# Summing softmax weights on GpSimd into one buffer per step, and single tiles on TensorE in gaps

## The chip, the cores and the metric

The kernel runs on one core of one Trainium2 chip. A core has engines that run side by side, each through its own list of instructions in order: TensorE (PE, matrix multiplication; its weight loads are shown apart as PEld), VectorE (DVE), ScalarE (ACT), GpSimd (POOL) and SyncE (SP, which here only issues DMA transfers). They wait for one another through semaphores. The metric is the device time of one execution in microseconds (us).

## The reference: what is computed

One pre-norm transformer layer in float32, for x of 2 x 2048 x 512:

```python
x = x + attention(layernorm(x))          # 16 heads of 32, rotary q and k, causal
x = x + ffn(layernorm(x))

# attention
scores = einsum('bhqd,bhkd->bhqk', q, k) / sqrt(dk)      # causal mask
attn   = softmax(scores, axis=-1)
ctx    = einsum('bhqk,bhkd->bhqd', attn, v)
return ctx @ Wo.T

# ffn: a base product, and 8 low-rank experts of rank 16, of which a router takes 2 per token
result = x @ base_w.T + base_b
gate   = top-2 of softmax(x @ router_w.T + router_b), renormalised
return result + 2.0 * sum over experts of gate * (x @ A_e) @ B_e
```

The change concerns the denominator of the softmax: for each query, the sum of exp(score - shift) over all keys.

## The kernel before

The 4096 tokens are cut into 8 blocks of 512 queries: blocks 0 to 3 are the first batch, 4 to 7 the second, and a block's place in its batch is j = 0 to 3. The heads come in 4 groups of four. A *step* is one block and one group (n, g), 32 in all. A step of place j has 4(j+1) tiles of 128 keys.

For one step, `row_maxima` first multiplies queries by keys in one orientation (tiles `sm`, L367) and VectorE takes the largest score of every query (`pm`, L375 and L380). Then `attend` multiplies keys by queries (tiles `sc`, L463), subtracts the maxima by a small multiplication (L471), and ScalarE writes the exponentials, the *weights*, into a tile buffer `pt` of 128 keys x 4 heads x 512 queries (L485). On the diagonal GpSimd sets the weights of later keys to zero (`affine_select`, L494). `weighted` (L519) multiplies weights by values into `av`. Of the four diagonal tiles, the second and the fourth share one buffer.

The denominator is made in two moves. When two neighbouring tiles both have had their `av` multiplication, GpSimd adds the second tile into the first (L534), in two halves of two heads. Three phases later (or two, in a gap) `summed` (L545) lets TensorE multiply the pair by a matrix of ones into the PSUM tile `den`. So a step of place j has 2(j+1) groups of four such multiplications, the last of them half as wide. After the last, ScalarE copies `den` out, the sums go through DRAM to spread them over partitions, VectorE takes reciprocals, and GpSimd multiplies them into `ctx` (L581).

Order. TensorE, ScalarE and VectorE run in the order in which the program writes their instructions; GpSimd and SP are ordered by the framework's scheduler. The program goes by *phases*. While the weights of one step are computed, the maxima of the next are computed beside them (`side_by_side`): one phase holds half of a weights tile and half of a maxima tile, or, where no maxima are left, a whole weights tile. After each phase `between` issues what is due (`av` two phases after the scores, `den` groups), then a list of other work is served: projections with their rotation (`project`, L185, L198 to L201), values (L210), and for finished blocks the output projection, router and feed-forward (`finish`, L239, L265, L320, L327). If a phase gave TensorE no such filler, `ahead` issues a `den` group early. The last step has no maxima beside it, and after it only the last block's `finish` remains.

`PTS = 4` buffers hold weights tiles; `before` sees to it that what reads the oldest has been issued. PSUM has six score banks in turn. `wo` and `base_w` (1 MB each) are loaded once and stay in SBUF.

Of the kernel before, what the change touches and what calls it, by code (L numbers as in the profile page):

```python
# [15 lines left out]
P = 128  # L16
# [5 lines left out]
BLK = 512  # L22
# [4 lines left out]
LORA_SCALING = 32.0 / 16.0  # L27
THETA = 10000.0
MASKED = -1e30
PTS = 4  # L30
SWAP = [i ^ 1 for i in range(32)]


# [1 line left out]
def preln_attention_moe_lora(  # L35
# [26 lines left out]


    et = mybir.EngineType
    ctx.enter_context(tc.manual_schedule(engines={et.PE, et.Activation, et.DVE}))


    banks = [0]
# [26 lines left out]

    blocks = [(b, j) for b in range(B) for j in range(NB)]

    def load_x(n, t, keep):
        b, j = blocks[n]
        if keep:  # L100
            xt = wide.tile([P, D], F32, tag="x", bufs=4, name=f"xf_{n}_{t}")
        else:
            xt = p2.tile([P, D], F32, tag="tmp", bufs=5, name=f"xa_{n}_{t}")
        nc.sync.dma_start(out=xt, in_=x[bass.ds(b * S + j * BLK + t * P, P), :])
        return xt
# [18 lines left out]
    wq = load_weight(wq_t, "wq")  # L124
    first_turn = load_turn(0)
    wv = load_weight(wv_t, "wv")
    wo = load_weight(wo_t, "wo")
    exp_in = load_weight(expert_in, "exp_in")
    bias_sb = const.tile([P, D + E], F32, name="bias_sb")
    nc.sync.dma_start(out=bias_sb, in_=bias.to_broadcast([P, D + E]))  # L130
    base_w = load_weight(base_wt, "base_w")
    exp_out = const.tile([ER, D], F32, name="exp_out")
    nc.sync.dma_start(out=exp_out, in_=expert_out)

    def moments(xt, t, name):

        n6, n2 = nc.vector.BN_STATS_DIM, nc.vector.BN_AGGR_DIM
        made = small.tile([P, n6 + n2 + 2], F32, tag="mom", bufs=4, name=f"mom_{name}_{t}")
        st, mv = made[:, :n6], made[:, n6 : n6 + n2]
        rstd, shift = made[:, n6 + n2 : n6 + n2 + 1], made[:, n6 + n2 + 1 :]  # L140
        nc.vector.bn_stats(st, xt)
        nc.vector.bn_aggr(mv, st)
        nc.gpsimd.tensor_scalar_add(rstd, mv[:, 1:2], EPS)
        nc.gpsimd.tensor_tensor(rstd, rstd, power, ALU.pow)
        nc.gpsimd.tensor_scalar(shift, mv[:, 0:1], rstd, -1.0, ALU.mult, ALU.mult)
        return rstd, shift
# [11 lines left out]
    def prepare(n):  # L158
# [23 lines left out]
        def project(which, w, g):  # L182
            pj = bank(f"{which}ps_{n}_{g}")
            for c in range(NC):
                nc.tensor.matmul(  # L185
                    out=pj,
                    lhsT=w[:, c, bass.ts(g, P)],
                    rhs=held["xn_t"][:, c, :],
                    start=(c == 0),
                    stop=(c == NC - 1),  # L190
                )
            if which == "k":
                dest = kv.tile([P, BLK], F32, tag="k", name=f"k_{n}_{g}")
            else:
                dest = wide.tile([P, BLK], F32, tag="q", bufs=3, name=f"q_{n}_{g}")
            made[which].append(dest)
            sw = p2.tile([P, BLK], F32, tag="tmp", bufs=5, name=f"sw_{which}_{n}_{g}")
            nc.vector.stream_shuffle(sw, pj, SWAP)  # L198
            nc.vector.tensor_mul(dest, pj, held["turn"][0])
            nc.gpsimd.tensor_mul(sw, sw, held["turn"][1])  # L200
            nc.gpsimd.tensor_add(dest, dest, sw)  # L201

# [24 lines left out]
    def finish(n, ctx_t):  # L227
# [3 lines left out]

        def load(t):
            held["x"].append(load_x(n, t, True))

        def output(t):
            xt = held["x"][t]
            po = bank(f"ops_{n}_{t}")
            for c in range(NC):
                nc.tensor.matmul(  # L239
                    out=po,  # L240
                    lhsT=ctx_t[c][:, bass.ts(t, P)],
                    rhs=wo[:, c, :],
                    start=(c == 0),
                    stop=(c == NC - 1),
                )
            nc.vector.tensor_add(xt, po, xt)
            held["by"].append(moments(xt, t, f"f{n}"))

        def scaled(t):
            xt = held["x"][t]  # L250
            xn = p2.tile([P, D], F32, tag="tmp", bufs=5, name=f"xn_f{n}_{t}")
            normalise(xn, xt, held["by"][t])
            held["xn"].append(xn)
            nc.gpsimd.tensor_add(xt, xt, bias_sb[:, :D])

        def turned(t):
# [59 lines left out]
        def result(t):  # L316
            xt = held["x"][t]
            po = bank(f"yps_{n}_{t}")
            for c in range(NC):
                nc.tensor.matmul(  # L320
                    out=po,
                    lhsT=held["xn_t"][:, c, bass.ts(t, P)],
                    rhs=base_w[:, c, :],
                    start=(c == 0),
                    stop=False,
                )
# [90 lines left out]
    def between():  # L417
# [4 lines left out]
            due.pop(0)[2]()  # L422
        return many > 0

    def ahead():

        for i, entry in enumerate(due):
            if entry[0] - entry[3] <= phase[0]:
                return due.pop(i)[2]()


    def attend(s):

# [3 lines left out]
        tiles = NT * (j + 1)  # L437
        together = [(kt,) for kt in range(diagonal + 1)]
        together += [(diagonal + 1, diagonal + 3), (diagonal + 2,)]
        pts, index, paired = {}, {}, {}  # L440

        def low(kt):
            return max(kt - diagonal, 0) * P
# [7 lines left out]
        def quad(*kts):  # L451
# [23 lines left out]

            def weigh(r):
                if kts[0] not in pts:
                    pt = p2.tile(
                        [P, 4, BLK], F32, tag="pt", bufs=PTS, name=f"pt_{n}_{g}_{kts[0]}"
                    )  # L480
                    for kt in kts:
                        index[kt], pts[kt] = begun[0], pt
                    begun[0] += 1
                pt = pts[kts[0]]
                nc.scalar.activation(  # L485
                    pt[:, r, all_of], sc[r][:, all_of], AF.Exp, scale=1.0 / math.sqrt(DK)
# [1 line left out]
                if kts[0] >= diagonal and r % 2:  # L488
# [2 lines left out]
                    on = pt[:, r - 1 : r + 1, at : at + len(kts) * P]  # L491
                    if len(kts) > 1:
                        on = on.rearrange("p h (k q) -> p h k q", q=P)
                    nc.gpsimd.affine_select(  # L494
                        out=on, in_=on, compare_op=ALU.is_ge, fill=0.0, base=0,
                        pattern=[[0, 2]] + [[0, len(kts)]] * (len(kts) > 1) + [[1, P]],
# [2 lines left out]

            def before():  # L500

                while any(tile <= begun[0] - PTS for _, tile, _, _ in due):
                    due.pop(0)[2]()

            def after():

                oldest = diagonal + 1 if kts[0] == tiles - 2 else kts[0] - kts[0] % 2
                later(2, index[oldest], lambda: weighted(kts))

            return before, take, scores, shift, weigh, after  # L510

        def weighted(kts):
            if kts[0] == 0:
                s["av"] = ps_o.tile([P, BLK], F32, tag="av", name=f"av_{n}_{g}")
            for kt in kts:
                jj, tt = divmod(kt, NT)
                for r in range(4):
# [5 lines left out]
                        start=(kt == 0),  # L523
                        stop=(kt == tiles - 2),
                    )

            for kt in kts:
                kt -= kt % 2
                paired[kt] = paired.get(kt, 0) + 1
                if paired[kt] == 2:  # L530
                    lo = low(kt + 1)
                    for r in (0, 2):
                        some = pts[kt][:, r : r + 2, place(kt, lo)]
                        nc.gpsimd.tensor_add(some, some, pts[kt + 1][:, r : r + 2, place(kt + 1)])  # L534
                    later(3, index[kt], lambda kt=kt: summed(kt), 1)
            if kts[-1] == tiles - 2:
                s["dest"] = wide.tile([P, BLK], F32, tag="ctx", bufs=6, name=f"ctx_{n}_{g}")
                nc.scalar.copy(s["dest"], s["av"])

        def summed(kt):  # L540
            lo = low(kt)
            if kt == 0:
                s["den"] = ps_o.tile([P, BLK], F32, tag="den", name=f"den_{n}_{g}")
            for r in range(4):
                nc.tensor.matmul(  # L545
                    out=s["den"][DK * r : DK * r + DK, lo:],
                    lhsT=ones,
                    rhs=pts[kt][:, r, lo:],
                    start=(kt == 0),
                    stop=(kt == tiles - 2),  # L550
                )
            if kt == tiles - 2:
                total = p2.tile([P, BLK], F32, tag="tmp", bufs=5, name=f"sum_{n}_{g}")
                nc.scalar.copy(total, s["den"])
                if (n, g) == steps[-1]:
# [14 lines left out]
                    nc.sync.dma_start(out=few, in_=spread(sums))  # L570

                def over_sums():
                    if (n, g) != steps[-1]:
                        nc.vector.reciprocal(few, few)
                        nc.sync.dma_start(out=spread(over), in_=few)
                        for r in range(4):
                            nc.sync.dma_start(
                                out=total[DK * r : DK * r + DK, :],
                                in_=over[r : r + 1, :].to_broadcast([DK, BLK]),
                            )  # L580
                    nc.gpsimd.tensor_mul(s["dest"], s["dest"], total)  # L581
                    s["ctx"].append(s["dest"])

                if (n, g) == steps[-1]:
                    over_sums()
                else:
                    set_aside(phase[0] + 4, over_sums)

# [107 lines left out]

    def end_block(n):

        start = phase[0] + 6
        end = max(begin[NC * (n + 2)] - EARLY, start + 24)  # L700
        stages = finish(n, contexts[n])
        for i, stage in enumerate(stages):
# [7 lines left out]
    for step in steps + [None]:  # L710
# [18 lines left out]
        for i in range(slots):  # L729
# [2 lines left out]
            todo = part(maxima, i, slots), late if i == 0 else part(weights, i - 1, slots)  # L732
            for _ in side_by_side(*todo):
                phase[0] += 1
                given = between()
                if ending is not None and len(contexts[ending]) == NC:
                    end_block(ending)
                    ending = None
# [9 lines left out]
                while waiting and waiting[0][2] <= phase[0]:  # L748
# [9 lines left out]
                    free = us > 0.0 and free  # L758
                    do_stage(waiting.pop(0)[3])
                    credit -= us  # L760
                    given = given or us > 0.0
                if not given:
                    ahead()
        late = part(weights, slots - 1, slots)
        if step:
            split()
            before, turned = s, turned_next
    for _ in side_by_side([], late):
        phase[0] += 1
        between()  # L770
    while due:
        due.pop(0)[2]()
    while aside:
# [54 lines left out]
```

## Time and profile before

| | us |
|---|---|
| median of 3 runs | 1978.18 (1974.35 to 1980.91) |
| the profiled execution's own time | 1982.82 |
| its span in the profile | 1981.0 |
| mean granted TensorE clock | 0.987 of full speed |

| engine, idle before a group of instructions | us in all | times | longest |
|---|---|---|---|
| ACT, exponentials, for TensorE's scores | 882.0 | 475 | 7.3 |
| POOL, adds L534, for ScalarE's exponentials | 193.6 | 45 | 10.6 |
| POOL, adds L534, for TensorE's `av` | 140.0 | 48 | 6.7 |
| POOL, `ctx` product L581, for a transfer | 84.8 | 25 | 10.0 |
| PEld, loads for `av`, for masks L494 | 32.4 | 40 | 1.7 |
| PE, `av`, for masks L494 | 14.2 | 28 | 1.3 |

The span is what the profiler recorded from first to last instruction; the profiled execution is one execution, a little over the median. A matrix multiplication in float32 shows as two instructions on TensorE, so a group of four is eight. Matmuls are pipelined and their ends are modelled: the share of busy time counts overlapped and stretched instructions too. In a timeline a row gives start, length, engine, line, operation, what is written from what, how many, and in brackets the engine's idle time before it with what ended it.

### The profile page before, as it was taken

To read this page: it belongs to the slowest core of one execution; us is meant where nothing else is said; L and a number is where in the kernel's file an instruction comes from. 1 tells how busy PE (TensorE), PEld (TensorE's weight loads), DVE (VectorE), ACT (ScalarE), POOL (GpSimd) and SP (SyncE) were. 2 spreads that over 40 slices of the span, in tenths; PEclk is the share of its full clock that TensorE was granted. 3 is DMA by queue.
4 is the path that set the end of the run, shared out by engine and by line. 5 is a ranking of instruction groups with operands and counts; after the bars stand their busy time and mean duration, and the time that the engine had idled before them with its cause. 6 is when DMAs were issued, how large, how long until landed. Compare 5 with 4: busy or idle time off the path is not lost.

```text
span 1981.0 us, 31399 instructions
## 1 busy us (share of the span) xinstructions
PE 1918.0 (97%) x12256; PEld 731.2 (37%) x12256; DVE 1018.2 (51%) x2760; ACT 768.0 (39%) x1601; POOL 1008.7 (51%) x906
## 2 busy tenths in 40 slices
PE   7999999999999999999999999999999999999997
PEld 3433433333333333333343434333433333333333
DVE  3555555555554655553255546446565555555403
ACT  1323342344433444353532334224434334443451
POOL 3545554455464555355565345435555545553572
PEclk9999999999999999999999999989999999999999
DMA  5000110000100000100000001100011000001000
GB/s 186 23 12 13 32 35 22 7 7 28 60 1 7 7 1 18 48 23 8 10 28 12 28 28 38 49 7 7 2 38 49 1 6 7 1 7 44 6 7 22
DMA packets 34861, 46.33 MB, mean 23 GB/s; under 512 B 12956, under 2 KB 13468, under 8 KB 34712
## 3 DMA queue, kind: packets, MB, share of 16 engines
q1 hardware_dynamic: 34712, 44.32, 7.0%
q8 instruction: 96, 1.57, 0.3%
q14 instruction: 53, 0.43, 0.1%
HBM read 35.40 MB, written 8.90 MB: 22 GB/s over the span
## 4 chain that ended last, share of the span: by engine, by line
PE 83%; POOL 7%; issue 4%; DVE 4%; ACT 1%; DMA 1%; SPq 0%; POOLq 0%; DVEq 0%
PE sm L367 24%; PE av L519 13%; PE den L545 6%; PE ops L239 6%; PE vps L210 6%; PE qps L185 5%; PE kps L185 5%; PE yps L320 5%; PE sc L471 5%; PE sc L463 4%; POOL pt L534 3%; POOL pt L494 2%; PE mid L265 1%; PE yps L327 1%; ACT pt L485 1%
## 5 line engine op out<-in xcount | busy, mean ns | idle before, releaser
L485 ACT ACTIVATE pt<-sc 128x512 f32<-128x512 f32 (+1 forms) x1152 | 595.1, 572 | 950.8 <-PE sc L471 882.0
L534 POOL TENSOR_TENSOR pt<-pt,pt 128x1024 f32<-128x1024 f32 (+2 forms) x320 | 609.9, 1920 | 339.2 <-ACT pt L485 193.6
L463 PE MATMUL sc<-q,k 32*128 32x512 f32 (+3 forms) x2560 | 677.5, 576 | 10.7 <-DVE parts L392 10.1
L367 PE MATMUL sm<-k,q 32*128 32x512 f32 (+3 forms) x2560 | 644.1, 574 | 6.3 <-POOL q L201 3.6
L380 DVE TENSOR_REDUCE pm<-sm 128x1 f32<-128x512 f32 x768 | 490.8, 685 | 286.5 <-PE sm L367 273.6
L367 PEld LDWEIGHTS sm<-k,q 32*128 32x128 f32 x2560 | 221.4, 184 | 375.0 <-issue 148.7
L519 PE MATMUL av<-pt,v 128*32 128x512 f32 (+3 forms) x2560 | 306.0, 550 | 19.1 <-POOL pt L494 14.2
L375 DVE CUSTOM_DVE_ANT_0 sm<-sm,mask 128x128 f32<-128x128 f32 (+3 forms) x512 | 245.8, 512 | 141.8 <-PE sm L367 118.7
L471 PE MATMUL sc<-max,ones_b 3*128 3x512 bf16 (+3 forms) x1280 | 261.2, 346 | 0.0
L463 PEld LDWEIGHTS sc<-q,k 32*128 32x128 f32 x2560 | 233.1, 185 | 51.2 <-issue 24.2
L494 POOL TENSOR_SCALAR_AFFINE_SELECT pt<-pt 128x256 f32<-128x256 f32 (+1 forms) x192 | 93.0, 485 | 154.7 <-ACT pt L485 152.2
L545 PE MATMUL den<-pt,ones 128*32 128x512 f32 (+1 forms) x1280 | 163.3, 569 | 0.0
L519 PEld LDWEIGHTS av<-pt,v 128*32 128x32 f32 x2560 | 57.5, 109 | 201.5 <-issue 142.1
L185 PE MATMUL kps<-xnt_a,wk 128*128 128x512 f32 x256 | 123.3, 626 | 5.0 <-ACT xnt_a L156 4.9
L239 PE MATMUL ops<-wo,ctx 128*128 128x512 f32 x256 | 120.2, 614 | 2.7 <-POOL ctx L581 2.7
L320 PE MATMUL yps<-base_w,xnt_f 128*128 128x512 f32 x256 | 116.9, 599 | 2.6 <-DVE pm L380 1.6
L185 PE MATMUL qps<-xnt_a,wq 128*128 128x512 f32 x256 | 118.3, 605 | 0.0
L210 PE MATMUL vps<-wv,xnt_a 128*128 128x512 f32 x256 | 117.5, 604 | 0.0
L471 PEld LDWEIGHTS <-ones_b 3*128 3x128 bf16 x1280 | 78.3, 94 | 101.0 <-issue 94.5
L200 POOL TENSOR_TENSOR sw_q<-sw_q,sin 128x512 f32<-128x512 f32 x32 | 40.7, 1273 | 112.5 <-DVE sw_q L198 112.5
L200 POOL TENSOR_TENSOR sw_k<-sw_k,sin 128x512 f32<-128x512 f32 x32 | 40.7, 1273 | 109.2 <-DVE sw_k L198 93.8
L581 POOL TENSOR_TENSOR ctx<-ctx,sum 128x512 f32<-128x512 f32 x32 | 40.6, 1268 | 90.1 <-DMA sum<-over 84.8
(85 smaller groups left out, 1246.4 us busy)
## 6 DMA issues: line engine op xcount, KB each, us to landing
xa<-in_x SPq DMA_DIRECT2D x32, 256.0 KB
xf<-in_x SPq DMA_DIRECT2D x32, 256.0 KB
out<-xf SPq DMA_DIRECT2D x32, 256.0 KB
sum<-over SPq DMA_DIRECT2D x124, 64.0 KB
cos<-in_cos SPq DMA_DIRECT2D x8, 256.0 KB
sin<-in_sin SPq DMA_DIRECT2D x8, 256.0 KB
sums<-sum SPq DMA_DIRECT2D x124, 2.0 KB
wk<-in_wk_t SPq DMA_DIRECT2D x1, 1024.0 KB
```

The costliest lines, as they stand in the source:

```text
L185: nc.tensor.matmul(out=pj, lhsT=w[:, c, bass.ts(g, P)], rhs=held["xn_t"][:, c, :], start=(c == 0), stop=(c == NC - 1),)
L210: nc.tensor.matmul(out=pv, lhsT=held["xn_t"][:, c, bass.ts(t, P)], rhs=wv[:, c, :], start=(c == 0), stop=(c == NC - 1),)
L239: nc.tensor.matmul(out=po, lhsT=ctx_t[c][:, bass.ts(t, P)], rhs=wo[:, c, :], start=(c == 0), stop=(c == NC - 1),)
L367: nc.tensor.matmul(out=sc[r][:, some[i]], lhsT=q[rows, bass.ts(ts[i], P)], rhs=keys[c][rows, : wide_of[i]], start=True, stop=True,)
L375: nc.vector.tensor_tensor_reduce(sc[r][:, here], sc[r][:, here], mask[:, BLK - w :], 1.0, 3.0 * MASKED, ALU.add, ALU.max, pm[:, t, r, c : ...
L380: nc.vector.reduce_max(pm[:, t, r, c : c + 1], sc[r], axis=AX.X)
L463: nc.tensor.matmul(out=sc[r][:, place(kts[i])], lhsT=keys[jj][rows, bass.ts(tt, P)], rhs=q[rows, low(kts[i]) :], start=True, stop=False,)
L471: nc.tensor.matmul(out=sc[r][:, place(kts[i])], lhsT=ones_b[rows, :], rhs=s["max"][rows, low(kts[i]) :], start=False, stop=True,)
L485: nc.scalar.activation(pt[:, r, all_of], sc[r][:, all_of], AF.Exp, scale=1.0 / math.sqrt(DK))
L519: nc.tensor.matmul(out=s["av"][rows, low(kt) :], lhsT=values[jj][g][:, tt, rows], rhs=pts[kt][:, r, place(kt)], start=(kt == 0), stop=(kt ...
L534: nc.gpsimd.tensor_add(some, some, pts[kt + 1][:, r : r + 2, place(kt + 1)])
L545: nc.tensor.matmul(out=s["den"][DK * r : DK * r + DK, lo:], lhsT=ones, rhs=pts[kt][:, r, lo:], start=(kt == 0), stop=(kt == tiles - 2),)
```

## The change

GpSimd joins the engines that run in the order written out. Each step has one buffer for the sum: the first tile of the step now lies in a buffer of its own (tag `acc`, two of them), and all other tiles of the step are added into it (`add`), one half at a time. The tile buffers go from 4 to 3.

When an add is issued is decided by a running estimate, `load_of`, of how many microseconds of work TensorE and GpSimd have been given. `keep_up`, at the end of each phase, issues adds of tiles at least three phases old while GpSimd's estimate is below TensorE's. `ahead`, in a phase without other filler, takes a tile that has not been added at all and lets TensorE multiply it by ones alone. `before` forces out what still holds the oldest buffer. Three phases after the last `av`, `summed` issues the adds that are left and one last multiplication, of the sum buffer.

The `ctx` product is set four phases later than the transfers that it needs, and a block's `finish` starts two phases after its contexts are complete instead of six. To make room, `wo` and `base_w` share one buffer and are loaded anew for each block: `wo` with the block's first x tile, `base_w` after its last output projection.

```diff
-PTS = 4
+PTS = 3
-    ctx.enter_context(tc.manual_schedule(engines={et.PE, et.Activation, et.DVE}))
+    ctx.enter_context(tc.manual_schedule(engines={et.PE, et.Activation, et.DVE, et.Pool}))
+    load_of = {"pool": 0.0, "pe": 0.0}
+    def pool_takes(us):
+        load_of["pool"] = max(load_of["pool"], load_of["pe"] - 4.0) + us
...
-    wo = load_weight(wo_t, "wo")
-    base_w = load_weight(base_wt, "base_w")
+    def load_in_turn(src, name):
+        w = wide.tile([P, NC, D], F32, tag="w", name=name)
+        nc.sync.dma_start(out=w, in_=src.rearrange("(c p) o -> p c o", p=P))
+        return w
...
+    unsummed = []
+    def add_up():
+        entry = unsummed[0]
+        pool_takes(entry["cost"])
+        entry["add"](entry["left"].pop(0))
+        if not entry["left"]:
+            unsummed.pop(0)
+    def keep_up():
+        while unsummed and unsummed[0]["first"][0] and load_of["pool"] < load_of["pe"]:
+            if unsummed[0]["phase"] + 3 > phase[0]:
+                break
+            add_up()
     def ahead():
-        for i, entry in enumerate(due):
-            if entry[0] - entry[3] <= phase[0]:
-                return due.pop(i)[2]()
+        for i, entry in enumerate(unsummed):
+            if (
+                len(entry["left"]) == 2 and entry["phase"] + 2 <= phase[0]
+                and entry["whole"]
+            ):
+                unsummed.pop(i)["multiply"]()
+                load_of["pe"] += 1.0
+                return
...
             def before():
-                while any(tile <= begun[0] - PTS for _, tile, _, _ in due):
+                last = begun[0] + 1 - PTS
+                while kts[0] and any(tile <= last for _, tile, _, _ in due):
                     due.pop(0)[2]()
+                while kts[0] and unsummed and unsummed[0]["tile"] <= last:
+                    if unsummed[0]["first"][0]:
+                        add_up()
+                    else:
+                        unsummed.pop(0)["multiply"]()
...
-            for kt in kts:
-                kt -= kt % 2
-                paired[kt] = paired.get(kt, 0) + 1
-                if paired[kt] == 2:
-                    lo = low(kt + 1)
-                    for r in (0, 2):
-                        some = pts[kt][:, r : r + 2, place(kt, lo)]
-                        nc.gpsimd.tensor_add(some, some, pts[kt + 1][:, r : r + 2, place(kt + 1)])
-                    later(3, index[kt], lambda kt=kt: summed(kt), 1)
             if kts[-1] == tiles - 2:
                 s["dest"] = wide.tile([P, BLK], F32, tag="ctx", bufs=6, name=f"ctx_{n}_{g}")
                 nc.scalar.copy(s["dest"], s["av"])
+                later(3, 1 << 30, summed)
+        def add(kt, r):
+            some = pts[0][:, r : r + 2, low(kt) :]
+            nc.gpsimd.tensor_add(some, some, pts[kt][:, r : r + 2, place(kt)])
+        def multiply(pt, last):
+            begins = s["den"] is None
+            if begins:
+                s["den"] = ps_o.tile([P, BLK], F32, tag="den", name=f"den_{n}_{g}")
+            for r in range(4):
+                nc.tensor.matmul(
+                    out=s["den"][DK * r : DK * r + DK, :], lhsT=ones, rhs=pt[:, r, :],
+                    start=begins, stop=last,
+                )
+        def summed():
+            while unsummed and unsummed[0]["den"] is s:
+                add_up()
+            multiply(pts[0], True)
...
-        start = phase[0] + 6
+        start = phase[0] + 2
...
+                keep_up()
```

## The prediction

> **What bounds the kernel now.** I read the busy shares and the chain of waits, then the groups by shape, then TensorE's timeline in a steady stretch, around the short step in the middle, and at the end.
>
> ```profile
> PE 1918.0 (97%) x12256; PEld 731.2 (37%) x12256; DVE 1018.2 (51%) x2760; ACT 768.0 (39%) x1601; POOL 1008.7 (51%) x906
> ...
> PE 83%; POOL 7%; issue 4%; DVE 4%; ACT 1%; DMA 1%; SPq 0%; POOLq 0%; DVEq 0%
> ```
>
> TensorE looks full, GpSimd half empty. The groups by shape (count, then busy us and mean ns) price both:
>
> ```profile
> L534 POOL TENSOR_TENSOR pt<-pt,pt 128x1024 f32<-128x1024 f32 x192 | 448.9, 2354 | 279.9 <-ACT pt L485 193.6 <-PE av L519 86.0
> ...
> L545 PE MATMUL den<-pt,ones 128*32 128x512 f32 x1024 | 143.0, 613 | 0.0
> ...
> L534 POOL TENSOR_TENSOR pt<-pt,pt 128x768 f32<-128x768 f32 x64 | 116.0, 1812 | 6.8 <-PE av L519 1.5
> ...
> L534 POOL TENSOR_TENSOR pt<-pt,pt 128x256 f32<-128x256 f32 x64 | 45.0, 725 | 52.5 <-PE av L519 52.5
> ```
>
> But 97% is no saturation. Two stretches of the timeline (start, length), TensorE's lines and one of VectorE:
>
> ```profile
> 1655.81 0.69 PE L367 MATMUL sm<-k,q 32*128 32x512 f32 x1
> ...
> 1656.97 2.60 DVE L380 TENSOR_REDUCE pm<-sm 128x1 f32<-128x512 f32 x4 [1.00 <-PE sm L367]
> ...
> 1659.11 1.07 PE L519 MATMUL av<-pt,v 128*32 128x512 f32 x8
> 1660.11 0.69 PE L367 MATMUL sm<-k,q 32*128 32x512 f32 x1
> ...
> 1661.39 1.06 PE L545 MATMUL den<-pt,ones 128*32 128x512 f32 x8
> 1662.39 0.69 PE L367 MATMUL sm<-k,q 32*128 32x512 f32 x1
> ...
> 1663.68 1.06 PE L519 MATMUL av<-pt,v 128*32 128x512 f32 x8
> 1664.67 0.69 PE L367 MATMUL sm<-k,q 32*128 32x512 f32 x1
> ```
>
> Two phases without a `den` group take 1660.11-1655.81 = 4.30 us; two with one take 1664.67-1660.11 = 4.56 (one phase holds half of a tile's scores and half of a maximum's; `av` fills every second one). The group fills 1.00 us (1661.39 to 1662.39), yet without it only 0.26 us goes: the next scores wait until VectorE has reduced the banks they reuse (four reductions back to back, 2.60 us).
>
> **The change, part by part.** Counts are from the changed program's instruction order.
>
> *TensorE's sums.* Before: 128 groups of four 512-wide multiplications and 32 of 256, 144 full ones. After: 113 full ones (32 final, 81 single tiles). Leaving out the last step (7.5 against 1), 136.5 become 112, 24.5 fewer. Some 20 fill phases that also hold maxima, at 0.26; 4.5 stand in phases of weights alone, where no reduction covers them, at 0.99: 5.2+4.5 = 10 us saved. Bounds: 24.5 x 0.26 = 6 and 24.5 x 0.99 = 24; I stay near 6, since most phases have maxima. The Trainium skill (Perfetto Trace Analysis, Identifying the Most-Contended Engine) says that matmul busy time is a bad measure of how near TensorE is to its limit; whoever takes the 97% as work would book 24 us here.
>
> *GpSimd's sums.* 192 adds of 1024 become 222; the 64 of 768 and 64 of 256 stay; 64 of 512 come in, priced by the other 128x512 tensor-tensor of this engine (1.27 us, L581). 30 x 2.354 + 64 x 1.27 = 152 us more, 1009 to 1161, 59% of the span. On average that fits. What matters is where TensorE waits for it.
>
> *The final multiplication (`summed`).* TensorE reaches it in program order, five phases after the last scores; it needs every add of its step. The last tile's adds are issued at the end of the third phase, and in many steps after a rotation (L200, L201) issued in that same phase. GpSimd now takes them in that order. The rotation's price, from the stretch around the short step:
>
> ```profile
> 992.66 3.70 PE L185 MATMUL qps<-xnt_a,wq 128*128 128x512 f32 x8
> ...
> 996.29 0.58 PE L367 MATMUL sm<-k,q 32*128 32x384 f32 x1
> ...
> 997.32 1.27 POOL L200 TENSOR_TENSOR sw_q<-sw_q,sin 128x512 f32<-128x512 f32 x1 [4.00 <-DVE sw_q L198]
> ...
> 998.68 1.26 POOL L201 TENSOR_TENSOR q<-q,sw_q 128x512 f32<-128x512 f32 x1
> ```
>
> The projection ends at T = 996.29 and the rotation at 999.94, T+3.65. With the last tile's two adds (2 x 1.27) GpSimd ends at T+6.3. TensorE needs only scores (1.3), `av` (1.0) and scores (1.3): T+3.6. It waits 2.7 us. That order stands in five steps (block, group: 0,3; 1,3; 2,3; 5,3; 6,3): 13.5. In (3,0) and (7,0) two adds of the tile pair (1.81+0.73 for a half) come after the rotation too: T+8.75, 5.1 each, 10.3. In (3,3) the second rotation starts at 1003.25 and ends at 1005.85; behind it stand 5.1 of the pair, 2.5 of the last tile and a 0.64 mask: 1014.1, against 1003.5 where the old trace has its last group there: 10.6. In (4,0): rotation to 1021.0, mask, 7.6 of adds, 1029.3 against 1022.1: 7.2. In (4,1) rotation, moments and three adds end 7.7 late. (1,1) issues three adds right before the multiplication, 4; (0,0) 1.9. Together 55. What queues behind it on TensorE is everything: next scores, so ScalarE's exponentials and VectorE's maxima. But these catch up meanwhile; up to 0.5 us comes back after each of 13 waits: 49. Bounds: 15 (only the three worst, halved) and 62.
>
> *Three tile buffers (PTS 4 to 3, two for the sum).* In step (3,3), whose weights run mostly alone, ten tiles are added whole: 10 x 4.7 + two rotations 5.1 + one 1.3 = 53 us from about 924 on, against about 60 in which TensorE needs them; with the rotations' waits I take +5, bounds 0 and 10.
>
> *The last step.* No maxima, and no tile is multiplied alone (`ahead` isn't called there). Before:
>
> ```profile
> 1881.13 4.68 POOL L534 TENSOR_TENSOR pt<-pt,pt 128x1024 f32<-128x1024 f32 x2 [6.68 <-ACT pt L485]
> ...
> 1931.07 0.59 ACT L554 COPY sum<-den 128x512 f32<-128x512 f32 x1 [1.71 <-PE den L545]
> ```
>
> The adds begin when tile 1 is there and end 49 us later (1929.9), seven and a half pairs of tiles in all. After: 12 tiles x 2 x 2.354 = 56.5, the pair 5.1, the last 2.5, masks 2.9, one `ctx` product 1.3: 68.3 us in one chain through one buffer. Three masks stand between adds and wait for exponentials that the add just before releases (ScalarE's four take 2.06): 1.7+1.5+0.8 = 4. 1881.1+72.3, plus the group 1.0, is 1954.5 against 1931: +24. Bounds 18 (no mask waits, start two us earlier) and 28. All behind it (`ops`, router, output) moves by as much. VectorE is idle in that stretch. The Trainium skill (GPSIMD Engine Reference, Performance versus the Vector engine) measures a tensor-tensor addition 1.96 times faster on VectorE and advises it there; by that page an estimate of the chain is 33 us for the 64 of adds, and the end would not move. This change does the opposite.
>
> *Masks, rotations, moments now in program order.* TensorE's waits for masks are 14.2 us in all before (L519 on L494); a mask may now wait behind an add (2.35) or come sooner. I take -5, bounds -14 and +20 (the 28 waits by 0.7).
>
> *Weights `wo` and `base_w` loaded per block,* 14 more 1 MB loads on SP. The opening moves 380 GB/s, so 2.8 us each plus some 2 until it lands (the first x, issued at 0.79, is used at 3.54). `base_w` has 10 us in the last block (`ops` end 1949.7, first use 1959.6), more elsewhere; `wo` is issued as soon as the previous block's last multiplication frees the buffer. Behind a waiting load on SP stand x loads and the reciprocals' transfers, with phases to spare. Cost 0; if one load in two were uncovered, 8 x 5 = 40. I keep 10 for the range.
>
> *The `ctx` product* moves four phases later, its transfers on SP stay, and the block's end starts four phases sooner: 0. GpSimd's 84.8 us of idle before it (25 waits for a transfer) may shrink, which is worth something only where a mask stands behind it; that is in the -5.
>
> **Sum:** -10+49+5+24-5 = +63. The profiled execution took 1982.8 us (span 1981.0), 4.6 (0.2%) over the median of the runs, 1978.2; 63 on the median is **2041 us**.
>
> **Rivals.**
> *A (forecast, 0.57):* waits at the final multiplications and the longer last step; 2015 to 2068.
> *B (0.20):* the waits in the run are hidden (GpSimd is ahead there, 41% idle), only the end grows: -10+24 = +14, 1992, to 2010. For it: the average load. Against: the rotation's T+3.65 stands in the trace.
> *C, the other side (0.06):* TensorE's own time counts in full: 24 saved, the mask waits gone (14, and 32.4 that its weight loads show before `av` for L494), less the end: -70+24 = -46, 1932, or 1965 with half of it. It decides if the final waits stay under some 20 us and the phase falls by 1.0 and not 0.26 per group; the 4.30/4.56 pair speaks against it.
> *D (0.13):* GpSimd in order also holds up rotations and moments, so scores and normalisations wait: +20 there, 10 from loads, 62 in place of 49: 63+20+10+13 = +106, 2084.
> *E, the change does little (0.04):* 81 single multiplications against the text's "only in gaps" means that nearly as much stays on TensorE (step (7,2) gets 13 groups for 7.5), and the end's cost meets C's saving: 1978.
>
> **How the numbers follow.** A measurement here tells 0.3%, 6 us, from no change. Slower holds A, B, D: 0.90; the same E, 0.04; faster C, 0.06. The range reaches from B's 1992 to past A, 2072, leaving out C, E and most of D.
>
> **What would show it.** In the new profile: TensorE idle before `den` for GpSimd's add, some 13 times, 3 to 10 us each, near 50 in all; the last step's adds back to back for about 70 us; span after the last group unchanged at 50 us; GpSimd 1160 busy. I am wrong if `den` shows under 20 us of waits, or the phase without a group falls well below 4.30 for two.

## The result, and the profile after

The changed kernel takes 2134.07 us (median of 4 runs, 2129.94 to 2136.76) against 1978.86 us (4 runs, 1974.35 to 1980.91): ratio 1.0786, 95% interval 1.0758 to 1.0814. That is 155 us more, where 63 were forecast and 2072 was the top of the range. The profiled execution took 2131.73 us. Times and ratios leave out runs in the chip's slower state, in which the same program ran longer at a lower clock; this concerns one of the four runs of e11.

The page's head, its chain of waits, and the granted clock by core:

```profile
PE 1964.7 (92%) x11880; PEld 731.1 (34%) x11880; DVE 1017.9 (48%) x2760; ACT 768.8 (36%) x1601; POOL 1151.5 (54%) x1000
...
PE 74%; POOL 16%; DVE 5%; issue 4%; ACT 1%; DMA 0%; DVEq 0%; POOLq 0%; ACTq 0%
...
core 0: 2130.0 us, clock 0.947
```

GpSimd's busy time is as forecast (1160), but its share of the chain went from 7% to 16%, and the clock from 0.987 to 0.947. TensorE's waits (who, for whom, us in all, times, longest):

```profile
PE den L599 <- POOL pt L591: 65.4, 27, 10.2
PE av L575 <- POOL pt L538: 34.0, 19, 5.5
PE sc L505 <- DVE parts L410: 17.4, 9, 2.2
PE sc L505 <- ACT pt L528: 9.7, 12, 1.2
...
PE sm L385 <- ACT pt L528: 5.7, 1, 5.7
```

The first line is the forecast's: 10.2 us of it in the last step, 55.2 in the run. The second was 14.2 us before.

Now the clock. The records of the granted clock hold two values, 1.0 and 0.5. TensorE's timeline around one of the mask waits, then three windows around it (window, length, busy us and count by engine, granted clock, DMA share, GB/s):

```profile
964.91 0.75 PE L505 MATMUL sc<-q,k 32*128 32x256 f32 x8
965.45 0.33 PE L513 MATMUL sc<-max,ones_b 3*128 3x256 bf16 x4
970.00 1.94 PE L575 MATMUL av<-pt,v 128*32 128x384 f32 x16 [4.23 <-POOL pt L538]
...
975.87 2.28 PE L505 MATMUL sc<-q,k 32*128 32x512 f32 x8
977.74 0.84 PE L513 MATMUL sc<-max,ones_b 3*128 3x512 bf16 x4
978.50 1.94 PE L575 MATMUL av<-pt,v 128*32 128x512 f32 x8
...
982.41 1.06 PE L575 MATMUL av<-pt,v 128*32 128x512 f32 x8
```

```profile
955.00:965.00 10.00, 9.54 (x78) 3.93 (x78) 5.95 (x22) 3.28 (x7) 9.92 (x8) 1.00 0.01 2
970.00:980.00 10.00, 10.00 (x60) 3.04 (x60) 0.00 (x0) 4.68 (x11) 8.11 (x8) 0.50 0.00 0
982.50:992.00 9.50, 9.50 (x40) 3.33 (x41) 2.08 (x7) 3.63 (x7) 3.96 (x3) 1.00 0.02 4
```

TensorE stands 4.23 us, then works at half clock until 982: a group for `av` takes 1.94 us at 978.50 and 1.06 at 982.41. So the wait costs its length and again some of it. In the stretch at half clock the page still shows TensorE fully busy.

What TensorE waited for stands in GpSimd's timeline at the same place:

```profile
961.54 1.27 POOL L213 TENSOR_TENSOR sw_k<-sw_k,sin 128x512 f32<-128x512 f32 x1
962.89 1.27 POOL L214 TENSOR_TENSOR k<-k,sw_k 128x512 f32<-128x512 f32 x1
964.12 4.65 POOL L591 TENSOR_TENSOR pt<-pt,pt 128x1024 f32<-128x1024 f32 x2
968.72 1.95 POOL L538 TENSOR_SCALAR_AFFINE_SELECT pt<-pt 128x512 f32<-128x512 f32 x4
```

A rotation (L213, L214) and two adds, 4.65 us, stand in front of the masks (L538).

With the clock's records laid over TensorE's busy time the span splits in three: idle; half of the busy time at half clock, which I call lost; and the rest. (Half is a little much: the group above took 1.94 us in place of 1.06, 0.88 more, and half of 1.94 is 0.97.)

| us | before | after | difference |
|---|---|---|---|
| span | 1981.0 | 2130.0 | +149.0 |
| TensorE idle | 63.0 | 165.2 | +102.2 |
| lost at half clock (50.3 and 184.1 us busy at half clock) | 25.2 | 92.1 | +66.9 |
| rest | 1892.8 | 1872.6 | -20.2 |

By stretch: up to the last transposition of maxima on TensorE (L397, now L415), where the last step's weights begin to run alone, 129.2 us more (1871.1 to 2000.3); from there to the last `den` group 21 more (59.9 to 80.8); behind it 48.9 against 50.0. Ahead of the last step idle time grew by 92.5 and the loss at half clock by 52, the rest fell by 15. The other 15 us lost at half clock lie in the last step, where GpSimd's chain of adds sets the end, so that they probably cost nothing.

### The profile page after: what moved, and what is told of

It reads as the page before. It is cut to its first block, busy times and chain, and to the rows that moved or that the text cites. A ratio compares the mean times of both kernels' runs of the same rounds, so it can differ in the third digit from the quotient of the medians.

```text
span 2130.0 us, 30782 instructions
## 1 busy us (share of the span) xinstructions
PE 1964.7 (92%) x11880; PEld 731.1 (34%) x11880; DVE 1017.9 (48%) x2760; ACT 768.8 (36%) x1601; POOL 1151.5 (54%) x1000
## 4 chain that ended last, share of the span: by engine, by line
PE 74%; POOL 16%; DVE 5%; issue 4%; ACT 1%; DMA 0%; DVEq 0%; POOLq 0%; ACTq 0%
PE sm L385 22%; PE av L575 11%; POOL pt L591 10%; PE den L599 6%; PE yps L338 5%; PE vps L223 5%; PE ops L254 5%; PE kps L197 5%; PE qps L197 5%; PE sc L513 4%; PE sc L505 3%; PE yps L345 1%; POOL sw_k L213 1%; POOL pt L538 1%; DVE sm L393 1%
## 5 line engine op out<-in xcount | busy, mean ns | idle before, releaser
L591 POOL TENSOR_TENSOR pt<-pt,pt 128x1024 f32<-128x1024 f32 (+3 forms) x414 | 756.1, 1847 | 59.2 <-ACT pt L528 54.2
L505 PE MATMUL sc<-q,k 32*128 32x512 f32 (+3 forms) x2560 | 700.5, 599 | 27.3 <-DVE parts L410 17.4
L575 PE MATMUL av<-pt,v 128*32 128x512 f32 (+3 forms) x2560 | 313.4, 573 | 34.9 <-POOL pt L538 34.0
L513 PE MATMUL sc<-max,ones_b 3*128 3x512 bf16 (+3 forms) x1280 | 266.1, 357 | 0.0
L505 PEld LDWEIGHTS sc<-q,k 32*128 32x128 f32 x2560 | 237.9, 193 | 82.3 <-ACT pt L528 29.3
L538 POOL TENSOR_SCALAR_AFFINE_SELECT pt<-pt 128x256 f32<-128x256 f32 (+1 forms) x192 | 92.3, 485 | 299.9 <-ACT pt L528 299.7
L599 PE MATMUL den<-pt,ones 128*32 128x512 f32 x904 | 153.6, 652 | 65.4 <-POOL pt L591 65.4
L213 POOL TENSOR_TENSOR sw_k<-sw_k,sin 128x512 f32<-128x512 f32 x32 | 40.7, 1272 | 217.3 <-DVE sw_k L210 201.9
L213 POOL TENSOR_TENSOR sw_q<-sw_q,sin 128x512 f32<-128x512 f32 x32 | 40.8, 1274 | 94.3 <-DVE sw_q L210 94.3
L155 POOL TENSOR_SCALAR mom_f<-mom_f 128x1 f32<-128x1 f32 x32 | 7.3, 227 | 145.3 <-DVE mom_f L153 135.8
```

The lines of the kernel that those rows point to most:

```text
L505: nc.tensor.matmul(out=sc[r][:, place(kts[i])], lhsT=keys[jj][rows, bass.ts(tt, P)], rhs=q[rows, low(kts[i]) :], start=True, stop=False,)
L513: nc.tensor.matmul(out=sc[r][:, place(kts[i])], lhsT=ones_b[rows, :], rhs=s["max"][rows, low(kts[i]) :], start=False, stop=True,)
L575: nc.tensor.matmul(out=s["av"][rows, low(kt) :], lhsT=values[jj][g][:, tt, rows], rhs=pts[kt][:, r, place(kt)], start=(kt == 0), stop=(kt ...
L591: nc.gpsimd.tensor_add(some, some, pts[kt][:, r : r + 2, place(kt)])
L599: nc.tensor.matmul(out=s["den"][DK * r : DK * r + DK, :], lhsT=ones, rhs=pt[:, r, :], start=begins, stop=last,)
```

## The experiments

Two theories stood at first. *One:* TensorE waits for GpSimd (final multiplications, masks, last step), and each wait is paid again in clock. *Two:* GpSimd or memory is simply loaded too much, waits and clock are symptoms. Ratios are to the kernel before, with 95% intervals.

**e1, the waits filled.** Multiplications by zeros in front of nine final multiplications.

```diff
+FILL = {(1, 1): 5, (2, 0): 2, (3, 0): 3, (3, 3): 9, (4, 0): 8, (4, 1): 6, (6, 0): 2, (7, 0): 3, (7, 3): 10}
         def summed():
...
+            for _ in range(FILL.get((n, g), 0)):
+                multiply(wk, False, zeros)
```

> Changed kernel, with multiplications by a tile of zeros put on TensorE in place of nine of its waits at the final multiplication (48 groups of about 1 us; they add 0 to den, and GpSimd's work is as before). Theory 1, the granted clock falls after idle stretches and this is a large part of the loss: half-clock time falls from 228 us to 150-190, the span by 10 to 25 us, to 2105-2124 of 2134. Theory 2, the clock has nothing to do with the waits, time went to GpSimd's load alone: half-clock time unchanged within 20 us and the span the same or up to 10 us longer (2134-2144).

2123.4 us, ratio 1.0722 (1.0697 to 1.0746). Half-clock time fell from 228 to 153 us, the span to 2116.3: with more instructions on TensorE and the same on GpSimd the kernel is 11 us faster (13.7 by the spans), within theory one. Ahead of the last step the zeros add 38 us of work (the rest) where 34 us of idle time go, which alone would be 4 us more; 17 us less are lost at half clock, and the stretch is 13 us shorter. The clock is a cause and not a symptom, but only a part was taken back.

**e2 and e5, the last step's tiles on TensorE.** In the last step, whole tiles go to `multiply` in place of `add_up`. e2 had this in the final loop alone; the adds had already been issued where `before` wants a tile buffer, so it took one tile of 12. e5 has it in `before` too, and keeps `keep_up` out of that step.

```diff
-                    if unsummed[0]["first"][0]:
+                    alone = (n, g) == steps[-1] and unsummed[0]["whole"]
+                    if unsummed[0]["first"][0] and not (alone and len(unsummed[0]["left"]) == 2):
                         add_up()
```

> Changed kernel, but in the last step the 12 whole tiles are multiplied by TensorE one by one instead of being added up by GpSimd. Theory 1, the last step is GpSimd's chain of 79 us where TensorE's own work is about 50: the last group moves from 80 us after the stretch's start to about 52-57, the time to 2105-2112. Theory 2, the last step is held by exponentials and tile buffers (3 instead of 4): at most 8 us come back, 2126-2134.

> Changed kernel, but all 12 whole tiles of the last step are multiplied by TensorE, where the run of e2 took only one (the others had been added before, where a tile buffer was wanted). Theory 1, the last step is GpSimd's chain: the step's stretch falls from 80 us to 52-58, the time to 2107-2114 of 2134. Theory 2, the stretch is held by exponentials and buffers: at most 8 us, 2126-2134.

e2: 2127.27 us, ratio 1.0742 (1.0724 to 1.0760), which tells nothing, since it did not do what it was for. e5: 2104.46 us, 1.0631 (1.0601 to 1.0660), 30 us less, with the stretch from the last transposition at 55.9 us in place of 80.8: theory one, and a little more than it had. GpSimd in the last step of the changed kernel:

```profile
2000.29 44.56 POOL L591 TENSOR_TENSOR pt<-pt,pt 128x768 f32<-128x768 f32 x22
2044.81 1.26 POOL L640 TENSOR_TENSOR ctx<-ctx,sum 128x512 f32<-128x512 f32 x1
2046.03 4.65 POOL L591 TENSOR_TENSOR pt<-pt,pt 128x1024 f32<-128x1024 f32 x2
2051.93 0.41 POOL L538 TENSOR_SCALAR_AFFINE_SELECT pt<-pt 128x256 f32<-128x256 f32 x1 [1.25 <-ACT pt L528]
...
2066.98 12.19 POOL L591 TENSOR_TENSOR pt<-pt,pt 128x1024 f32<-128x1024 f32 x8
```

The first row opens with six adds of the step before, 7.6 us by e5, where they stand alone. So this step's own chain runs from 2007.9 to 2079.2: 71.3 us, where 72.3 were forecast.

**e3, the final multiplication later.**

```diff
-                later(3, 1 << 30, summed)
+                long = tiles > NT and (n, g) != (NB - 1, NC - 1)
+                later(6 if long else 4, 1 << 30, summed)
```

The edit has two further parts: a single tile may not go ahead while an older sum is open, and the reciprocals come 3 + 3 phases later in place of 4 + 4.

> Changed kernel, with the final multiplication issued 6 phases after the last av in long steps and 4 in short ones, in place of 3 (its reciprocals 3+3 phases later in place of 4+4). Theory 1, the waits before den and the clock after them: the den waits outside the last step fall from 55 to 15-30 us (the short steps 3,3 to 4,1 keep most of theirs), half-clock time falls by 30 to 60 us, time 2080-2115. Theory 2, GpSimd simply has too much to do in order, so that the wait only moves to masks, exponentials and tile buffers: 2125-2140.

2055.88 us, 1.0377 (1.0358 to 1.0395): 78 less, more than theory one had it. Idle fell by 38, the loss at half clock by 17, the rest by 18; TensorE has 100 groups in place of 113, which may account for most of the last. Outside the last step only 8 us before `den` remain, but 41 us before masks.

**e4, the loads alone.** The kernel before, with `load_in_turn` for `wo` and `base_w`.

> Kernel before, with nothing but wo and base_w loaded per block into one shared buffer (14 more 1 MB loads). Theory 1 (prediction's term 0): 1978-1984, TensorE's waits for ops and yps under 5 us. Rival, the loads are late or crowd SP's queue: waits before ops or yps of 2 to 5 us in each of 8 blocks, 2000-2020.

1983.04 us, 1.0017 (1.0002 to 1.0031), as theory one had it: at most 6 us, below what this measurement tells from no change.

**e6 and e7, GpSimd's order.** e6 is the changed kernel with the scheduler's order on GpSimd, e7 the kernel before with program order and nothing else: one word, taken away or added.

```diff
-    ctx.enter_context(tc.manual_schedule(engines={et.PE, et.Activation, et.DVE, et.Pool}))
+    ctx.enter_context(tc.manual_schedule(engines={et.PE, et.Activation, et.DVE}))
```

> Changed kernel, with GpSimd's order again left to the scheduler, which may let masks, rotations and moments pass an add; all else as in the changed kernel. Theory 1, the order on GpSimd makes the waits: the masks' waits fall from 34 to 10-20 us, those before den from 65 to 30-50, time 2070-2105. Theory 2, it is one chain of adds through one buffer with its multiplication at a fixed phase, in whatever order: 2120-2145.

> Kernel before, with nothing but GpSimd put into program order. Theory 1 (order makes the waits): the pairs' adds stand before masks and behind rotations, TensorE waits 20 to 50 us more and the clock falls with it, 2010-2050. Theory 2 (order harmless by itself): 1975-1990.

e6: 2016.44 us, 1.0186 (1.0140 to 1.0231), 118 less than the changed kernel. e7: 2079.82 us, 1.0516 (1.0479 to 1.0552), 101 more than the kernel before. Both lie outside what either theory had.

In e6 TensorE and GpSimd issue what they issue in the changed kernel, and GpSimd is as busy (1157 us against 1152): it is the order, and not GpSimd's load, that costs the 118 us. TensorE's largest wait for GpSimd in e6:

```profile
PE av L575 <- POOL pt L538: 50.4, 49, 2.4
```

No wait before `den` is left among TensorE's seven largest. The masks' waits grew to 50.4 us, but they are 49 with 2.4 the longest, where the changed kernel has 19 and 5.5. In program order GpSimd stands until its next instruction can go: for VectorE's part of rotations and moments it stood 488 us in the changed kernel (L213 and L155), 314 before and 310 in e6. Of the 65.4 us of waits before `den` 44, and of the 34.0 for masks 31, end a busy stretch of GpSimd that began with such a wait for VectorE. That these waits, and then the adds, hold up the sums and masks behind them is read from the trace; no run takes the rotations alone out of the order.

e7 has another wait in the same place. TensorE's waits for GpSimd, and GpSimd's own largest wait in e7 and the same one before:

```profile
PE av L519 <- POOL pt L494: 48.9, 33, 6.5
PE den L545 <- POOL pt L534: 22.9, 19, 3.3
```

```profile
POOL ctx L581 <- DMA sum<-over: 237.1, 28, 20.6
```

```profile
POOL ctx L581 <- DMA sum<-over: 84.8, 25, 10.0
```

GpSimd around the longest of the masks' waits in e7, and the same instructions before:

```profile
206.14 1.26 POOL L581 TENSOR_TENSOR ctx<-ctx,sum 128x512 f32<-128x512 f32 x1 [6.47 <-DMA sum<-over]
207.36 0.41 POOL L494 TENSOR_SCALAR_AFFINE_SELECT pt<-pt 128x256 f32<-128x256 f32 x1
207.74 4.63 POOL L534 TENSOR_TENSOR pt<-pt,pt 128x1024 f32<-128x1024 f32 x2
212.33 1.01 POOL L494 TENSOR_SCALAR_AFFINE_SELECT pt<-pt 128x256 f32<-128x256 f32 x2
```

```profile
188.64 4.66 POOL L534 TENSOR_TENSOR pt<-pt,pt 128x1024 f32<-128x1024 f32 x2
193.26 0.41 POOL L494 TENSOR_SCALAR_AFFINE_SELECT pt<-pt 128x256 f32<-128x256 f32 x1
194.89 1.26 POOL L581 TENSOR_TENSOR ctx<-ctx,sum 128x512 f32<-128x512 f32 x1 [1.23 <-DMA sum<-over]
196.10 1.00 POOL L494 TENSOR_SCALAR_AFFINE_SELECT pt<-pt 128x256 f32<-128x256 f32 x2
```

In e7 the `ctx` product stands first in the order and waits 6.47 us for its transfer; the two adds, 4.63 us, and the masks come late behind it, and TensorE waits 6.5 us. The scheduler had put the same adds and one mask ahead of the product. Of e7's waits 22 of the 48.9 us for masks and 21 of the 22.9 before `den` end a busy stretch of GpSimd that began with a product waiting for its transfer. The changed kernel has its products four phases later, and none of its waits for masks or sums begins so. So e7 shows that program order costs the old kernel 101 us, but in good part through a wait that the changed kernel avoids; what the order costs the change is told by e6.

**e11 and e12, av of masked tiles a phase later.**

```diff
-                later(2, index[kts[0]], lambda: weighted(kts))
+                later(3 if kts[0] >= diagonal else 2, index[kts[0]], lambda: weighted(kts))
```

> Changed kernel with nothing but av of the masked tiles one phase later. Theory 1, the masks behind the adds are a term of their own (34 us of waits, with the half clock after them): the waits for masks fall to 10-18 us, the time by 20 to 45 us, 2090-2114. Theory 2, av is late anyway, the chain of adds holds the next tile: 2125-2140.

> Kernel before with nothing but av of the masked tiles one phase later. Theory 1: its 14 us of mask waits (and some of the 32 us that its weight loads show) go, 1960-1973. Theory 2, it moves the adds of the last tiles and with them the final multiplication: 1976-1990.

e11 (with the final multiplication kept at its phase): 2097.54 us, 1.0601 (1.0564 to 1.0637), 37 less, as theory one had it; TensorE's waits for masks fell from 34.0 to 4.9 us. But TensorE now waits 23.5 us before `sm` (19 times, 1.4 at most) and 23.4 before `sc` for exponentials (9.7 in the changed kernel). Ahead of the last step idle time fell by 13 and the loss at half clock by 16: the pauses became shorter more than fewer. The edit also moved 12 single tiles from TensorE to GpSimd (101 groups in place of 113), which may be the 6 us by which the rest fell. e12, the same in the kernel before: 2006.26 us, 1.0122 (1.0099 to 1.0145), slower than either theory had it. Its masks' waits went (2.2 us), 18.7 us of waits before `sm` came, and the rest grew by 12. There the pair's add hangs on the same phase; which of its followers pays stays open.

**e8, e9, e10, edits together.** e8 is e3 and e5, with the final multiplication of the last step but one left at three phases; e9 is e6 and e5; e10 is e9 with the edit of e11.

> Changed kernel with both edits: final multiplications 6 (4) phases after the last av as in e3, and the last step's 12 whole tiles multiplied by TensorE as in e5. Theory 1, the two losses add: 2055.9 less 20 to 27, 2029-2036, what is left over 1980 being the masks' waits (41 us in e3) and half-clock stretches. Theory 2: no more than e3, 2048-2056.

> Changed kernel with GpSimd's order left to the scheduler (as in e6) and the last step's 12 whole tiles multiplied by TensorE (as in e5). Theory 1, the order and the last step are two separate losses and with both gone the change is about even with the kernel before: 2016 less 22 to 30, 1986-1994. Theory 2, with a free order the last step's chain is hidden already or the edits overlap: 2003-2018.

> As e9, with av of the masked (diagonal) tiles issued one phase later (3 phases after the scores in place of 2; the final multiplication stays at its phase). Theory 1, the masks' waits are on the path: in e6 50 us before av; they fall under 20 and the time to 1955-1978, below the kernel before. Theory 2, TensorE only waits elsewhere instead (for tile buffers, for reductions): within 8 us of e9.

e8: 2033.68 us, 1.0262 (1.0225 to 1.0300). e9: 1992.06, 1.0069 (1.0044 to 1.0094). e10: 1975.84, 0.9970 (0.9942 to 0.9998), with 7.6 us of waits for masks. All three lie where their first theory had them. With the order free, the last step on TensorE and the masks out of the way, the new sums are even with the old, perhaps 0.3% better.

**e13, three tile buffers** in the kernel before (`PTS = 3`).

> Kernel before with three tile buffers in place of four, nothing else. Theory 1 (the prediction's term, 5, bounds 0 to 10): 1980-1990. Rival, the buffers are what holds the exponentials and with them TensorE's av: 1995-2030.

2195.95 us, 1.1078 (1.1043 to 1.1113), outside both. A pair holds two of the three buffers there; in the changed kernel the sum has buffers of its own. So this says that the old way cannot do with three, and nothing of the new one.

**e14 and e15, pauses alone.** The kernel before, GpSimd as it was: TensorE waits 31 times for ScalarE's copy of `den`; in e15 ScalarE repeats the copy three times.

```diff
                 nc.scalar.copy(total, s["den"])
+                if (n, g) != steps[-1]:
+                    for _ in range(3):          # e15 alone
+                        nc.scalar.copy(total, total)
+                    nc.tensor.matmul(out=s["den"][:DK, :], lhsT=zeros, rhs=total, start=True, stop=True)
```

> Kernel before, with one multiplication by zeros (into the den bank, after it has been read) on TensorE behind each of 31 copies of den, so that TensorE pauses for ScalarE's copy, 1 to 2.5 us each, 35 to 75 us of idle time in all; GpSimd's work is untouched. Theory 1, a pause costs its length and the half clock behind it: half-clock time rises from 52 us to 110-200, and the time by 1.3 to 1.8 times the added idle time, 2030-2100. Theory 2, the half clock belongs to GpSimd's load and not to pauses: half-clock time stays under 75 us and the time rises by the added idle time or less, 2010-2050.

> As e14 (kernel before with 31 pauses on TensorE, GpSimd's work untouched), but with ScalarE copying the sums onto themselves three times more before the multiplication by zeros, so that each pause is about 2.5 to 3.2 us. Theory 1, the length of the pause decides: most of the 31 are followed by a half-clock stretch, half-clock time 110-250 us, and the time grows over e14 (2029) by the 50 to 65 us of longer pauses and 25 to 70 us more for the clock, 2100-2165. Theory 2, it is not the pause: half-clock time under 75 us and 2075-2095.

e14: 2028.84 us, 1.0232 (1.0211 to 1.0254); e15: 2128.08, 1.0765 (1.0736 to 1.0793). e14 by itself went against theory one: its half-clock time fell, from 51 us to 38. So e15 made the same pauses longer; its time lies where theory one had it, its half-clock time, 109 us, at the lower edge. The waits and one place in each timeline, e14 first:

```profile
PE den L558 <- ACT sum L556: 32.2, 31, 1.2
...
538.72 1.04 PE L558 MATMUL den<-sum,zeros 128*32 128x512 f32 x2 [1.07 <-ACT sum L556]
539.69 0.69 PE L369 MATMUL sm<-k,q 32*128 32x512 f32 x1
...
core 0: 2029.0 us, clock 0.991
```

```profile
PE den L560 <- ACT sum L559: 92.7, 31, 3.1
...
570.25 1.75 PE L560 MATMUL den<-sum,zeros 128*32 128x512 f32 x2 [3.02 <-ACT sum L559]
571.93 1.22 PE L369 MATMUL sm<-k,q 32*128 32x512 f32 x1
...
575.15 0.69 PE L369 MATMUL sm<-k,q 32*128 32x512 f32 x1
...
core 0: 2122.3 us, clock 0.974
```

After 1.07 us the scores run at 0.69 us as ever; after 3.02 us they take 1.22. Of e14's 31 pauses none is followed by a half-clock stretch, of e15's 20 are. From e14 to e15 the span grows by 93.3: idle 60.3, half clock 34.0, rest -1.0. GpSimd's work is the same in both: the length of the pause decides.

The split for all runs that carry the argument:

| us | span | idle | half clock | rest |
|---|---|---|---|---|
| after | 2130.0 | 165.2 | 92.1 | 1872.6 |
| e1, filled | 2116.3 | 126.1 | 69.6 | 1920.6 |
| e3, later | 2056.2 | 127.2 | 74.8 | 1854.2 |
| e5, last step | 2103.0 | 152.8 | 75.7 | 1874.5 |
| e6, order free | 2006.2 | 106.5 | 51.5 | 1848.2 |
| e11, masks | 2092.9 | 155.2 | 70.2 | 1867.5 |
| e10, three edits | 1974.4 | 82.8 | 47.3 | 1844.3 |
| before | 1981.0 | 63.0 | 25.2 | 1892.8 |
| e7, order alone | 2077.9 | 124.1 | 49.9 | 1903.9 |

The rest is not pure work: e6 issues on TensorE what the changed kernel issues, and has 24 us less of it. Waits too short to show as idle may be in it; no run separates them.

## Why the prediction was wrong

The direction and the places were right; two steps of the sum failed. The larger is the price of a wait: "up to 0.5 us comes back after each of 13 waits: 49". Waits were booked at their length, less something. The runs show the opposite sign: behind a wait of some 2 us and more the clock mostly halves (the counts stand at the end). This term was not in the sum at all, and is +67 us here, 52 of them ahead of the last step. Three things carry it beside the trace of the changed kernel: e15 against e14, e1, and the kernel before itself, where 22 executions of one program go from 1973.9 us at a mean clock of 0.991 to 1985.2 at 0.985, 17.4 us per 0.01 by a straight line (correlation -0.97). From 0.987 to 0.947 that line makes 70; that is far beyond the clocks it was drawn from, so it agrees with 67 and proves nothing by itself.

The second is "I take -5, bounds -14 and +20" for masks, rotations and moments in program order. The masks' waits grew by 19.8 us, the very bound on the other side, and with them out of the way (e11) 37 us come back, 16 of them the clock ahead of the last step. The text saw that a mask may wait behind an add, and took it as even with those that come sooner. Rival D, GpSimd in order holding up more than the sums, was nearest to the mechanism. But it had scores and normalisations wait; the trace shows the masks waiting, and TensorE's wait for a rotation (`sm` for `q`) at 3.6 us, once, as before. And 2084 was too low for lack of the clock. e6 puts the order at 118 us in all, and its trace has them ahead of the last step (idle 56, half clock 38, rest 24). That is not a further term: the waits before `den` and the clock behind all the long waits are in it.

The other steps:

- TensorE's sums, -10 (bounds -6 to -24): 113 groups, the rest fell by 15 ahead of the last step. Within the bounds, as far as the rest measures it.
- GpSimd's sums, 1161: 1151.5.
- The final multiplication, 55 us of waits before anything comes back: 55.2. By place, with the forecast behind: (1,1) 5.6, 4; (3,3) 9.2, 10.6; (4,0) 8.2, 7.2; (4,1) 6.2, 7.7; (3,0) and (7,0) 3.8, 5.1; the five single ones 1.4, 2.7; (0,0) 1.0, 1.9. Not forecast: (5,1) 3.4, (2,0) and (6,0) 3.0 each, (1,0) 0.8. The large places were right; that the total is right is luck in part: 10 us at places not listed stand against 10 us too many at the others. Four of them:

```profile
289.55 1.07 PE L599 MATMUL den<-pt,ones 128*32 128x512 f32 x2 [5.61 <-POOL pt L591]
1079.84 1.92 PE L599 MATMUL den<-pt,ones 128*32 128x512 f32 x4 [9.24 <-POOL pt L591]
1107.11 2.29 PE L599 MATMUL den<-pt,ones 128*32 128x512 f32 x6 [8.18 <-POOL pt L591]
1141.19 2.29 PE L599 MATMUL den<-pt,ones 128*32 128x512 f32 x6 [6.22 <-POOL pt L591]
```

- Three tile buffers, +5 (0 to 10): ScalarE waits 108.5 us (38 times; before, 8.8 and 7) for adds to free a buffer, and TensorE's waits for exponentials grew by 15 us (9.7 and 5.7, against 0.4). Above the bound by the trace; no run separates it.
- The last step, +24 (18 to 28): +21, with the chain as long as forecast, 71.3 against 72.3. It starts 7.6 us after the last transposition, before it was 10.0. Behind the last group nothing grew, as forecast.
- Loads, 0: 2.7 us in e4, with an interval that almost reaches none.
- The `ctx` product and the end of a block, 0: not tried by themselves. e7, which has program order without the four phases, shows what the delay guards against: 237 us in which GpSimd stands for transfers, 40.8 in the changed kernel.
- Small slips in the sum change nothing: the list of final waits has 12 places and not 13, its three worst halved are 13 us and not 15, and the last step's chain makes 23.5 and not 24.

In sum, ahead of the last step: idle 92 where 49 were forecast (49, 5 and -5), half clock 52 where none was, and the rest -15 where -10 was.

## What to carry to other kernels

Price a wait on TensorE by its length and by the clock behind it, and look for both: idle time shows the first, and the granted clock by windows the second, under a busy share that looks full. An engine put into program order needs a place by hand for every small instruction that another engine waits for: a long instruction, or one that itself waits, in front of a short, urgent one costs more than the average load tells. Such an order can be tried by itself: here one word, taken out of the change, gave back 118 of its 155 us.

## What the hardware showed

Over the profiles of the two kernels and all fifteen runs, I took TensorE's pauses that begin at full clock and asked whether a half-clock stretch starts in the pause or within 3.4 us behind it:

| pause, us | 1.0-1.25 | 1.25-1.6 | 1.6-2 | 2-3 | 3-5 | over 5 |
|---|---|---|---|---|---|---|
| pauses | 92 | 150 | 71 | 118 | 78 | 37 |
| followed by half clock | 8 | 49 | 46 | 90 | 71 | 37 |

The stretches last 3.4 us or a multiple of it (3.4 to 20.5 in the changed kernel). The Trainium skill (TensorE: Matmul & The Clock Gate, What's actually happening) has the gate close after an idle window of about 3.4 us and open after a busy one. The multiples agree with such a window; the length does not: pauses of 1.25 to 1.6 us were followed by half clock in a third of the cases, and in e15 20 of 31 pauses of 2.7 to 3.1 us.
